# GAT's two sum tables laid out by a node's place in its block

## The chip, the cores and the metric

The kernel runs on one core of a Trainium2 chip. The metric is the device time of one execution in microseconds (us), from the first instruction to the last; lower is better. Three timed runs before the change gave 3942.16, 3943.05 and 3946.96 us, a median of 3943.05. One more execution was profiled, and the profile's lines are of that one.

A core has a matrix engine (PE; PEld is its loading of weights), a vector engine (DVE), a scalar engine (ACT), GpSimd (POOL) and SyncE (SP). Each works through its own queue of instructions in order. Transfers (DMAs) are issued from the queues of SP, ACT and POOL and carried by 16 DMA engines that all queues share.

## The reference, cut to what matters

A graph of 3125 nodes and 103125 edges passes through a layer norm, three GIN layers and a residual, then through a second layer norm and a diffusion block of three graph attention (GAT) layers with 8 heads. The change concerns the GAT layers alone. Each of them computes, for every node, a softmax over its incoming edges and the weighted sum of its neighbours' rows:

```python
xw = (x @ W).reshape(n_nodes, H, C)
logits = jax.nn.leaky_relu(al_s[src] + al_d[dst], LRELU_SLOPE)
m = jax.lax.stop_gradient(jax.ops.segment_max(logits, dst, num_segments=n_nodes))
e = jnp.exp(logits - m[dst])
denom = jax.ops.segment_sum(e, dst, num_segments=n_nodes)
alpha = e / denom[dst]
out = jax.ops.segment_sum(alpha[:, :, None] * xw[src], dst, num_segments=n_nodes)
```

A linear term of the layer's input is added, the result is normalized over all nodes, and a SiLU follows. The layers give 256, 256 and 128 features (D), with H = 8.

## The kernel before

Nodes are cut into NT = 25 blocks of Q = 125. A tile holds one block with a node on each partition, so "place in the block" is the partition. `search` and `slots` sort the graph at run time, and everything after that lies in `fast`, behind a branch on whether the graph fits.

**Index building (`slots`).** For each pair of blocks at most one edge per node goes into a regular part; the edges left over are kept per node in up to 48 slots (`RMAX`). For those, nodes are ranked by how many they have, and `perm` (L997) holds, for each rank, the node's number. Numbers of 3125 and more mark ranks without a node. Beside this, L961 on DVE builds the dense adjacency 1000 columns at a time into tiles `a`, with PE and ACT ahead of it, and ACT's queue stores them (`adj_rows`). After the last store POOL scatters left-over weights into `adj` with 400 indirect DMAs (L1015), and the GIN layers read the table.

**A GAT layer (`gat`).** It projects the nodes, stores a table of rows for gathering (`tab`) and the dense term (`dense`), and then calls `add_edges`, which forms two partial sums for each node, each with its own maximum and denominator (2H statistics):

- The regular part. For block t, with the nodes on the partitions, the sum goes into tile `o1`, and ACT's queue stores its 125 rows to the DRAM table `res` (L1330), which lies by node number. Its statistics stay on chip in `stat`.
- The left-over part. POOL gathers rows by `idx`; the sums of 128 ranked nodes and their statistics form `o2`, of D + 16 columns. POOL scatters its rows by `perm` to the DRAM table `more` (L1306 puts the scatter on a list), which also lies by node number.

Within `add_edges` the order of instructions is the order of the code (`manual_schedule`). Everywhere else a planner orders the instructions of each engine when the program is built.

**The close of a layer (`close_rows`).** ACT's queue reads the second sum's statistics from `more` into `back` (L1359). DVE combines them with `stat` (L1362 to L1371) into two factors for each node and head. Then, for seven groups of four blocks (the last has one), SP's queue loads four rows per partition from `res` and from `more` into `got1` and `got2` (L1380, four buffers each) and the dense term (L1388, eight buffers). DVE multiplies both by their factors (L1382) and adds them (L1385), PE adds the dense term (L1390) and the transposed sums (L1392) in PSUM, ACT copies to `xt` (L1396) and DVE takes statistics (L1397), once for each 128 features. Nothing of the next layer starts before the last statistics are there.

The loads and stores go through `by_rows` (L59 to L65), which issues one DMA for the first 112 of 125 partitions and a second one for the last 13; in the profile they all have the line L65. In the tables before, node (t, p) is row t * 125 + p, so the four rows that a partition needs lie 125 rows apart, and each is a piece of its own:

```python
res, more = (a[:N].rearrange("(t p) d -> p t d", p=Q) for a in (res, more))
by_rows(nc.scalar, back, more[:, :, D:])
...
        by_rows(nc.sync, a[:, :n], part[:, t0 : t0 + n, :D])
```

Of the kernel before, what the change touches and what calls it, by code (L numbers as in the profile page):

```python
# [10 lines left out]
F32 = mybir.dt.float32  # L11
BF16 = mybir.dt.bfloat16
I32 = mybir.dt.int32
AF = mybir.ActivationFunctionType
ALU = mybir.AluOpType
AX = mybir.AxisListType
# [3 lines left out]
P = 128  # L20
N = 3125
E = 103125
NT = 25
Q = 125
NP = NT * P
# [34 lines left out]
def by_rows(engine, out, in_):  # L60

    even = out.shape[0] // 16 * 16
    for rows in (slice(0, even), slice(even, out.shape[0])):
        if rows.start < rows.stop:
            engine.dma_start(out[rows], in_[rows])  # L65
# [559 lines left out]
class Fast(Base):  # L625
# [146 lines left out]
    def slots(self):  # L772


        nc, tc = self.nc, self.tc
        keep = self.keep
        self.perm = keep.tile([P, NT], I32, name="perm")
        self.idx = keep.tile([P, NT, RMAX], I32, name="idx")
        self.void = keep.tile([P, NT, NT + 1], F32, name="void")
# [15 lines left out]
        with tc.tile_pool(name="slots", bufs=1) as sp, tc.tile_pool(name="slots_ps", bufs=1, space=PSUM) as ps:  # L795
# [65 lines left out]
            for t, c in enumerate(spans):  # L861
                if t % 5 == 0:
                    keys(t, t + 5)
                n = CAPS[t]
# [11 lines left out]
            more = sp.tile([P, NT], F32, name="more")  # L876
# [38 lines left out]
            for t0 in range(0, NT, 4):  # L915
                n = min(4, NT - t0)
# [30 lines left out]
            with tc.tile_pool(name="build", bufs=1) as sp:  # L947

                for s in range(NT):
                    a = sp.tile([P, N], F32, name="a", bufs=3)[:Q]  # L950
                    for c0 in range(0, N, 8 * Q):
                        cols = [(c, min(4 * Q, N - c)) for c in range(c0, min(c0 + 8 * Q, N), 4 * Q)]
                        at = sp.tile([P, 2, 4 * Q], BF16, name="at_src", bufs=3)[:Q]
                        w = ps.tile([P, 2, BLK], F32, name="w", bufs=2)[:Q]
                        for i, (c, n) in enumerate(cols):
                            p = ps.tile([P, BLK], F32, name="by", tag="by", bufs=2)[:Q, :n]
                            nc.tensor.matmul(p, pick[0][:, s], by_src[:, c : c + n], start=True, stop=True)
                            nc.scalar.copy(at[:, i, :n], p)
                            nc.tensor.matmul(w[:, i, :n], pick[1][:, s], by_src[:, c : c + n], start=True, stop=True)
                        k = len(cols)  # L960
                        nc.vector.scalar_tensor_tensor(  # L961
                            a[:, c0 : c0 + k * n].rearrange("p (k n) -> p k n", k=k), at[:, :k, :n], self.own[:Q],
                            w[:, :k, :n], op0=ALU.is_equal, op1=ALU.mult,
                        )
                    by_rows(nc.scalar, self.adj_rows[s * Q : (s + 1) * Q], a)


                rows = sp.tile([P, NT, 2 * RMAX + 1], F32, name="rows_at")
                nc.sync.dma_start(rows, rows_d.rearrange("(t p) f -> p t f", p=P))
                there, vals, nodef = rows[:, :, :RMAX], rows[:, :, RMAX : 2 * RMAX], rows[:, :, 2 * RMAX]  # L970
                spare = sp.tile([P, NT, RMAX], F32, name="spare")
                for t in range(NT):
                    nc.gpsimd.iota(
                        spare[:, t], pattern=[[P, RMAX]], base=N * N + sum(MORE[:t]) * P, channel_multiplier=1,
                        allow_small_or_imprecise_dtypes=True,
                    )
                shape = [P, NT, RMAX]
                cell = sp.tile(shape, F32, name="cell")
                nc.vector.tensor_scalar(cell, there, -1.0, float(N), op0=ALU.add, op1=ALU.mult)
                nc.vector.tensor_tensor(cell, cell, nodef[:, :, None].to_broadcast(shape), op=ALU.add)  # L980
                nc.vector.tensor_sub(cell, cell, spare)
                some = sp.tile(shape, F32, name="some")

                nc.vector.memset(some[:, :, RMAX - 1], 0.0)
                nc.vector.tensor_tensor(
                    some[:, :, : RMAX - 1], there[:, :, : RMAX - 1], there[:, :, 1:], op=ALU.is_gt
                )
                nc.vector.tensor_mul(cell, cell, some)
                for t in range(NT):
                    m0 = sum(MORE[:t])  # L990
                    c = slice(m0, m0 + MORE[t])
                    nc.vector.tensor_tensor(celli[:, c], cell[:, t, : MORE[t]], spare[:, t, : MORE[t]], op=ALU.add)
                    nc.vector.tensor_copy(val[:, c], vals[:, t, : MORE[t]])
                    for q in range(c.start, c.stop):
                        self.scatter(self.adj, [(val[:, q : q + 1], celli[:, q : q + 1])], "adj")

                nc.vector.tensor_copy(self.perm, nodef)  # L997
                nc.vector.tensor_scalar(some, there, 0.0, float(N + 1), op0=ALU.is_equal, op1=ALU.mult)
                nc.vector.scalar_tensor_tensor(self.idx, there, -1.0, some, op0=ALU.add, op1=ALU.add)

# [88 lines left out]
    def gat(self, layer, K, D, xt, yt, ready):  # L1089


        nc, tc = self.nc, self.tc
        C, W, KO = D // H, D + H, D // P
        name = lambda n: f"L1_gnn_{n}{layer}"
        tab = tc.dram_tile([N + 1, W], F32, name=f"tab{layer}")
        ald_d = tc.dram_tile([NP, H], F32, name=f"ald{layer}")
        dense = tc.dram_tile([KO, P, NP], F32, name=f"gat_dense{layer}")
        res = tc.dram_tile([NP, D], F32, name=f"gat_res{layer}")
        more = tc.dram_tile([NP, D + 2 * H], F32, name=f"gat_more{layer}")
        with ExitStack() as ctx:  # L1100
            pool = ctx.enter_context(tc.tile_pool(name=f"gat{layer}", bufs=1))
# [10 lines left out]
            with tc.tile_pool(name=f"gat_sum{layer}", bufs=2) as io:  # L1112
                with tc.tile_pool(name=f"gat_ps_a{layer}", bufs=3, space=PSUM) as ps:
                    S = 4
                    for t0 in range(0, NT, S):
                        n = min(S, NT - t0)
                        ready(t0, n)
                        for t in range(t0, t0 + n):
                            p = ps.tile([P, BLK], F32, name="pw", tag="mm")[:Q, : W + H]
# [10 lines left out]
                    for c0 in range(0, N, BLK):  # L1130
                        w = min(BLK, N - c0)
                        for ko in range(KO):
                            p = ps.tile([P, BLK], F32, name="p1", tag="mm")
# [5 lines left out]
                            d = io.tile([P, BLK], F32, name="dense")  # L1139
# [9 lines left out]
    def add_edges(self, io, ps, layer, D, xt, yt, xw, ald, stat, tab, ald_d, res, more):  # L1149

        nc = self.nc
# [151 lines left out]

        def end_others(t, o, pa):
            nc.scalar.copy(o[:, :D], pa)
            late.append((more, [(o, self.perm[:, t : t + 1])], None))  # L1306


        load(0)
# [5 lines left out]
        for t in range(NT):  # L1315
            ahead = t + 1 < NT
            if t + 2 < NT:
                load(t + 2)
            nxt = parts(t + 1) if ahead else []
            pa = ps.tile([P, D], F32, name="pa1", tag="pa1")[:Q]  # L1320
            for i in range(3):
                if i == 1:

                    weighed = sum_others(copies - 8)
                if ahead:
                    gather(t + 1, *nxt[i])
                add_part(pa, e, *now[i])
            o = io.tile([P, D], F32, name="o1")[:Q]
            nc.scalar.copy(o, pa)
            by_rows(nc.scalar, res[t * Q : (t + 1) * Q], o)  # L1330
            added = weighed and add_others(*weighed)
            if ahead:
                now, e = nxt, weigh(t + 1, nxt)
            if added:
                end_others(*added)
# [18 lines left out]
    def close_rows(self, pool, io, ps, D, yt, stat, back, dense, res, more, bg, bb):  # L1354

        nc = self.nc
        C, KO = D // H, D // P
        res, more = (a[:N].rearrange("(t p) d -> p t d", p=Q) for a in (res, more))
        by_rows(nc.scalar, back, more[:, :, D:])  # L1359
        den1, top1, den2, top2 = stat[:, :, :H], stat[:, :, H:], back[:, :, :H], back[:, :, H:]  # L1360
        m = pool.tile([P, NT, H], F32, name="m")[:Q]
# [12 lines left out]
        for b, t0 in enumerate(range(0, NT, 4)):  # L1374
            n = min(4, NT - t0)
            c0, w = t0 * Q, n * Q
            given = []
            for name, part, s in (("got1", res, top1), ("got2", more, top2)):
                a = io.tile([P, 4, D], F32, name=name, bufs=4)[:Q]
                by_rows(nc.sync, a[:, :n], part[:, t0 : t0 + n, :D])  # L1380
                v = a[:, :n].rearrange("p t (h c) -> p t h c", c=C)
                nc.vector.tensor_tensor(v, v, s[:, t0 : t0 + n, :, None].to_broadcast([Q, n, H, C]), op=ALU.mult)  # L1382
                given.append(a)
            a = given[0]
            nc.vector.tensor_add(a[:, :n], a[:, :n], given[1][:, :n])  # L1385
            for ko in range(KO):
                d = io.tile([P, BLK], F32, name="dense", bufs=8)
                nc.sync.dma_start(d[:, :w], dense[ko, :, c0 : c0 + w])  # L1388
                p = ps.tile([P, BLK], F32, name="p1", tag="mm")
                nc.tensor.matmul(p[:, :w], self.ident, d[:, :w], start=True, stop=False)  # L1390
                for i in range(n):
                    nc.tensor.matmul(  # L1392
                        p[:, i * Q : (i + 1) * Q], a[:, i, ko * P : (ko + 1) * P], self.ident[:Q, :Q], start=False,
                        stop=i == n - 1,
                    )
                nc.scalar.copy(yt[ko][:, c0 : c0 + w], p[:, :w])  # L1396
                nc.vector.bn_stats(stats[:, ko, b], p[:, :w])  # L1397
# [132 lines left out]
```

## Time and profile before

| what | value |
|---|---|
| median of three runs | 3943.05 us |
| profiled execution | 3936.36 us |
| its span, first to last instruction | 3934.5 us |
| mean granted PE clock | 0.791 |
| busy: PE, DVE, POOL, ACT | 2175.0, 2211.1, 2011.1, 866.9 us |
| DMA | 557.74 MB, 142 GB/s over the span |
| first close, from `back`'s issue to its last statistics | 2318.0 to 2375.4 us |
| second close | 3159.5 to 3220.3 us |
| third close | 3873.6 to 3907.0 us |

All times inside the execution count from the start of the span. A line of the timeline gives start and length in us, the engine with the source line, the operation, what it writes and reads with shapes, how many were merged, and in brackets the idle time before it and what ended that. SPq and ACTq are the DMA issues of those queues: their length is the time that the queue took to issue, not the transfer. A line of the waits gives who waited, for what, the sum in us, how often, and the longest. Two lines of the page show how even the load is and where DMA stands over the span's 40 slices of 98 us:

```profile
PE 2175.0 (55%) x9841; PEld 1566.1 (40%) x9841; DVE 2211.1 (56%) x3558; ACT 866.9 (22%) x2127; POOL 2011.1 (51%) x1916
...
DMA  3000496960019993644444364555444356444323
```

### The profile page before, as it was taken

How to read it: one execution, taken by the hardware profiler on the slowest of the kernel's cores; microseconds unless marked ns; L12 is line 12 of the kernel's file. 1: busy time of each engine (PE TensorE's matmuls, PEld its weight loads, DVE VectorE, ACT ScalarE, POOL GpSimd, SP SyncE). 2: the span in 40 equal slices, each digit the busy share in tenths (PEclk: the TensorE clock that was granted, in tenths of full speed). 3: DMA queues.
4: the chain of work that ended last, by engine and by line, in shares of the span. 5: the costliest groups of instructions: out<-in, count | busy, mean ns of one | idle time of the engine just before them, and what ended most of it. 6: DMA issues, size and time to landing. Idle time of an engine off the chain costs nothing. (4 is left out here: it accounts for less than half of the span.)

```text
span 3934.5 us, 32038 instructions
## 1 busy us (share of the span) xinstructions
PE 2175.0 (55%) x9841; PEld 1566.1 (40%) x9841; DVE 2211.1 (56%) x3558; ACT 866.9 (22%) x2127; POOL 2011.1 (51%) x1916
## 2 busy tenths in 40 slices
PE   1001352000019997788898638788998355676533
PEld 0000120000003333567676525666776245665532
DVE  7799864210000002388898743788898553676544
ACT  0001353000000002333433204333443022222111
POOL 4512307677750000457667731476677704777772
PEclk8555685555559997899999868999999677888765
DMA  3000496960019993644444364555444356444323
GB/s 131 12 14 6 150 297 143 272 200 0 1 50 372 356 368 122 184 134 152 148 144 145 99 142 157 106 162 162 144 158 112 96 124 162 138 137 137 103 54 77
DMA packets 224866, 557.74 MB, mean 142 GB/s; under 512 B 90249, under 2 KB 135057, under 8 KB 208843
## 3 DMA queue, kind: packets, MB, share of 16 engines
q1 hardware_dynamic: 112634, 307.69, 23.8%
q0 software_dynamic: 74800, 158.73, 16.1%
q10 hardware_dynamic: 37250, 89.18, 7.4%
q8 instruction: 80, 1.31, 0.1%
q14 instruction: 102, 0.84, 0.1%
HBM read 439.37 MB, written 116.05 MB: 141 GB/s over the span
## 5 line engine op out<-in xcount | busy, mean ns | idle before, releaser
L1023 POOL DMA_INDIRECT rows<-tab,idx x1200 | 1266.5, 1055 | 626.6 <-issue 271.4
L1015 POOL DMA_INDIRECT adj<-val,celli x400 | 423.7, 1059 | 302.1 <-DMA gw<-in_L_gnn_gat_w 149.8
L1051 PE MATMUL pa<-adj_t,h 125*64 125x500 f32 (+1 forms) x1050 | 269.7, 554 | 511.5 <-DMA adj_t<-adj 510.8
L1221 PE MATMUL pa<-xt,ident 125*125 125x256 f32 (+1 forms) x1800 | 395.6, 376 | 239.4 <-DVE xt L1219 194.7
L1171 PE MATMUL g<-xw,hot 125*125 125x264 f32 (+1 forms) x2400 | 498.7, 360 | 37.5 <-ACT xt L1174 37.5
L1174 ACT COPY xt<-g 125x528 f32<-125x528 f32 (+1 forms) x700 | 439.8, 636 | 303.5 <-PE g L1171 296.5
L1221 PEld LDWEIGHTS pa<-xt,ident 125*125 125x125 f32 x1800 | 323.0, 212 | 302.9 <-DVE xt L1219 196.5
L1171 PEld LDWEIGHTS g<-xw,hot 125*125 125x125 f32 x2400 | 387.3, 192 | 128.1 <-ACT xt L1174 83.4
L1212 DVE TENSOR_TENSOR xt<-xt,le 125x3072 f32<-125x3072 f32 (+1 forms) x150 | 421.6, 2811 | 0.0
L1299 PE MATMUL pa<-rows,ident 128*128 128x256 f32 (+1 forms) x1236 | 289.1, 388 | 230.7 <-issue 186.7
L1023 POOL DMA_INDIRECT at<-ald,perm x75 | 74.7, 996 | 622.1 <-DMA ald<-ald 414.8
L170 DVE TENSOR_TENSOR h<-p,L_gnn_b 125x256 f32<-125x256 f32 (+1 forms) x21 | 8.3, 395 | 644.1 <-PE p L168 611.9
L1051 PEld LDWEIGHTS pa<-adj_t,h 125*64 125x64 f32 x1050 | 86.7, 137 | 673.8 <-issue 578.2
L1299 PEld LDWEIGHTS pa<-rows,ident 128*128 128x128 f32 x1236 | 228.9, 217 | 283.3 <-issue 194.9
L1171 PE MATMUL g<-xw,xt 125*125 125x264 f32 (+1 forms) x1350 | 289.5, 370 | 57.5 <-ACT xt L1174 32.8
L1212 DVE TENSOR_TENSOR rows<-rows,le 128x2048 f32<-128x2048 f32 (+8 forms) x180 | 292.8, 1627 | 0.0
L1171 PEld LDWEIGHTS g<-xw,xt 125*125 125x125 f32 x1350 | 226.1, 199 | 109.8 <-ACT xt L1174 59.3
L1219 DVE TENSOR_TENSOR xt<-xt 125x1536 f32<-125x1536 f32 (+1 forms) x150 | 223.8, 1492 | 5.1
L1351 ACT ACTIVATE le<-le 125x208 f32<-125x208 f32 (+16 forms) x147 | 42.9, 292 | 659.2 <-DVE le L1350 645.1
L1281 DVE TENSOR_TENSOR le<-rows,at 128x64 f32<-128x64 f32 (+4 forms) x162 | 35.9, 222 | 261.6 <-DMA rows<-tab,idx 224.8
L1063 ACT COPY gin_acc<-pa 128x500 f32<-128x500 f32 (+1 forms) x21 | 10.2, 531 | 770.9 <-DMA adj_t<-adj 523.6
L1297 DVE TENSOR_TENSOR rows<-rows 128x1024 f32<-128x1024 f32 (+5 forms) x174 | 157.0, 902 | 6.0
(268 smaller groups left out, 2779.3 us busy)
## 6 DMA issues: line engine op xcount, KB each, us to landing
hot<-hot SPq DMA_DIRECT2D x48, 1562.5 KB
adj_t<-adj SPq DMA_DIRECT2D x144, 500.0 KB
adj_t<-adj SPq DMA_DIRECT2D x72, 562.5 KB
xt<-hot SPq DMA_DIRECT2D x24, 1562.5 KB
adj<-a ACTq DMA_DIRECT2D x25, 1367.2 KB
hot<-one ACTq DMA_DIRECT2D x25, 1367.2 KB
rows<-tab,idx POOLq DMA_INDIRECT x1200
row<-lane_d SPq DMA_DIRECT2D x25, 683.6 KB
```

Of the source, the lines that this page charges most:

```text
L1015: st = self.nc.gpsimd.indirect_dma_start(out=table, out_offset=bass.IndirectOffsetOnAxis(ap=idx, axis=0), in_=row, in_offset=None)
L1023: self.nc.gpsimd.indirect_dma_start(out=out, out_offset=None, in_=table, in_offset=bass.IndirectOffsetOnAxis(ap=idx, axis=0))
L1051: nc.tensor.matmul(pa[i * D0 : (i + 1) * D0, c // B, :w], h[:, s], tiles[i][:, c : c + w], start=s0 == 0, stop=s0 + i >= NT - 2 and i == 1,)
L1171: nc.tensor.matmul(g[:Q, j // k, j % k * W : (j % k + 1) * W], one, xw[:, t if s == NT else s], start=True, stop=True)
L1174: nc.scalar.copy(rows[:, i : i + m].rearrange("p (b k) w -> p b k w", k=k), g[:Q, :banks, : k * W].rearrange("p b (k w) -> p b k w", w=W),)
L1212: nc.vector.tensor_tensor(r, r, e[:, s0 : s0 + n, :, None].to_broadcast([*r.shape[:3], C]), op=ALU.mult)
L1219: nc.vector.tensor_add(rows[:, :m, :D], rows[:, :m, :D], rows[:, m:n, :D])
L1221: nc.tensor.matmul(pa, self.ident[:Q, :Q], rows[:, j, :D], start=s0 + j == 0, stop=s0 + n == NS and j == m - 1)
L1281: nc.vector.tensor_tensor(l[:, k0 : k0 + n], rows[:, :n, D:], at[:, None, :].to_broadcast([P, n, H]), op=ALU.add)
L1297: nc.vector.tensor_add(rows[:, : n - m, :D], rows[:, : n - m, :D], rows[:, m:n, :D])
L1299: nc.tensor.matmul(pa, self.ident, rows[:, k, :D], start=k0 + k == 0, stop=k0 + n == MORE[t] and k == m - 1)
L1351: nc.scalar.activation(e, l, AF.Exp)
```

## The change

Row numbers in both tables are turned round: node (t, p) becomes row p * 25 + t. `res` is declared as [Q, NT, D], and block t is stored to `res[:, t]`, a row of D numbers every 25 rows. The scatter to `more` uses new row numbers, `turned`. They are made once in `slots` from the node number n: with t the number of multiples of 125 up to n, the new row is n + 24 n - 3124 t, which is 25 (n - 125 t) + t; numbers from 3125 on stay. In the close, the four rows of a partition are then adjacent in memory. For `more` the load takes whole rows with their 16 statistics columns, so that they stay one piece, and the tile `got2` grows to D + 16 columns, of which the first D are used. `back` is still read as 16 columns of each row.

```diff
+        self.turned = keep.tile([P, NT], I32, name="turned")
...
                 nc.vector.tensor_copy(self.perm, nodef)
+
+                bounds = sp.tile([P, NT], F32, name="bounds")
+                nc.gpsimd.iota(bounds, pattern=[[Q, NT]], base=Q, channel_multiplier=0, allow_small_or_imprecise_dtypes=True)
+                past = some[:, :, :NT]
+                nc.vector.tensor_tensor(
+                    past, nodef[:, :, None].to_broadcast([P, NT, NT]), bounds[:, None, :].to_broadcast([P, NT, NT]),
+                    op=ALU.is_ge,
+                )
+                turned = sp.tile([P, NT], F32, name="turned_f")
+                off = sp.tile([P, NT], F32, name="off")
+                nc.vector.reduce_sum(turned, past, axis=AX.X)
+                nc.vector.tensor_scalar(off, turned, -(NT * Q - 1.0), None, op0=ALU.mult)
+                nc.vector.scalar_tensor_tensor(off, nodef, NT - 1.0, off, op0=ALU.mult, op1=ALU.add)
+                nc.vector.tensor_scalar(turned, nodef, float(N), None, op0=ALU.is_lt)
+                nc.vector.tensor_mul(off, off, turned)
+                nc.vector.tensor_tensor(self.turned, nodef, off, op=ALU.add)
...
-        res = tc.dram_tile([NP, D], F32, name=f"gat_res{layer}")
+
+        res = tc.dram_tile([Q, NT, D], F32, name=f"gat_res{layer}")
...
-            late.append((more, [(o, self.perm[:, t : t + 1])], None))
+            late.append((more, [(o, self.turned[:, t : t + 1])], None))
...
-            by_rows(nc.scalar, res[t * Q : (t + 1) * Q], o)
+            by_rows(nc.scalar, res[:, t], o)
...
-        res, more = (a[:N].rearrange("(t p) d -> p t d", p=Q) for a in (res, more))
+        more = more[:N].rearrange("(p t) d -> p t d", p=Q)
...
-                a = io.tile([P, 4, D], F32, name=name, bufs=4)[:Q]
-                by_rows(nc.sync, a[:, :n], part[:, t0 : t0 + n, :D])
+                a = io.tile([P, 4, part.shape[2]], F32, name=name, bufs=4)[:Q]
+                by_rows(nc.sync, a[:, :n], part[:, t0 : t0 + n])
+                a = a[:, :, :D]
```

## The prediction

> **What bounds the kernel now.** No single engine does: DVE is busy 56% of the span, PE 55%, POOL 51%. The span is a chain of stages, so I read the page's 40 slices first, to find the stages, then each stage that the diff touches in the timeline, the waits and the packet records (each DMA packet's queue, size and time). Two places are touched: the end of the index building (around 457 us) and the close of each of the three GAT layers, where `res` and `more` are read back (2318 to 2376, 3159 to 3222, 3874 to 3907 us). First, what the DMA engines do there, beside a stretch of GIN (start:end, length, busy of PE, PEld, DVE, ACT, POOL, then PE clock, DMA share, GB/s):
>
> ```profile
> 1180.00:1300.00 120.00, 110.61 (x500) 43.17 (x497) 4.73 (x14) 7.70 (x14) 0.00 (x0) 1.00 0.99 369
> 2318.00:2363.00 45.00, 22.26 (x85) 14.35 (x86) 27.53 (x33) 5.25 (x10) 0.00 (x0) 0.73 1.05 219
> 3159.00:3204.00 45.00, 22.95 (x82) 14.90 (x82) 22.73 (x29) 5.07 (x10) 0.00 (x0) 0.64 1.02 218
> 3873.00:3898.00 25.00, 12.76 (x42) 7.27 (x42) 14.53 (x26) 2.94 (x6) 0.00 (x0) 0.65 0.97 201
> ```
>
> The DMA engines are full in each close, at 201 to 219 GB/s, where GIN's 4000-byte rows get 369. That looks like the thing to mend. But who waits for these loads? The waits of the second close, and one line of the whole run's:
>
> ```profile
> PEld p L1392 <- DVE got L1385: 23.3, 6, 6.6
> ...
> DVE stats L1397 <- ACT xt L1396: 15.0, 10, 2.7
> ...
> DVE m L1362 <- DMA back<-gat_more: 51.2, 3, 19.5
> ```
>
> DVE waits for ACT, PE for DVE, and DVE for one transfer only, `back`, once a layer. It never waits for `got`. The timeline of the first close says why:
>
> ```profile
> 2346.08 1.22 DVE L1385 TENSOR_TENSOR got<-got,got 125x1024 f32<-125x1024 f32 x1
> ...
> 2347.36 1.29 PEld L1392 LDWEIGHTS p<-ident,got 125*128 125x128 f32 x8 [4.56 <-DVE got L1385]
> ...
> 2348.98 0.57 ACT L1396 COPY xt<-p 128x500 f32<-128x500 f32 x1 [5.60 <-PE p L1392]
> ...
> 2352.55 0.69 DVE L1397 BATCH_NORM_STATS2 stats<-p 128x6 f32<-128x500 f32 x1 [2.28 <-ACT xt L1396]
> 2353.16 1.21 DVE L1382 TENSOR_TENSOR got<-got,back 125x1024 f32<-125x1024 f32 x1
> ```
>
> Add, transposes, copy, statistics, and only then the next block's second multiply: 7.5 us a block (two blocks from 2340.7 to 2355.7), in the fixed order of DVE's queue. By the packet records the loads arrive every 6.7 us: `got` of blocks 1, 3 and 5 is in at 2333.9, 2346.9 and 2360.5, and its second multiply runs at 2338.2, 2353.2 and 2369.0. The loads are 4 to 9 us ahead, and pull further ahead. **So a close lasts from the landing of `back` to the end of a chain of DVE, PE and ACT; the `got` loads are hidden.** What sets `back` is seen in the second layer:
>
> ```profile
> 3159.49 2.53 ACTq L65 DMA_DIRECT2D back<-gat_more  x2
> 3159.59 1.06 SPq L65 DMA_DIRECT2D got<-gat_res  x2
> 3160.70 0.85 SPq L65 DMA_DIRECT2D got<-gat_more  x2
> 3161.60 0.98 SPq L1388 DMA_DIRECT2D dense<-gat_dense  x2
> 3165.32 0.83 SPq L65 DMA_DIRECT2D got<-gat_res  x2
> ...
> 3170.15 0.37 DVE L1362 TENSOR_TENSOR m<-stat,back 125x200 f32<-125x200 f32 x1 [19.47 <-DMA back<-gat_more]
> ```
>
> 200 KB in 64-byte pieces take 10.7 us, with SP's loads beside them; in layers 0 and 2 it is 7.2 and 6.6 us.
>
> **Part 1, reads of `res` and `more` (L1380).** Removed: three of four packets. Per full block and table 500 rows of 1024 bytes (512 in layer 2) become 125 of 4096 and 4352 (2048 and 2304). The DMA count stays (two per load), SP's issue time (about 0.45 us each) with it; `more` brings its 16 statistics columns, 6% more bytes. [...] By the rows it is 0, since nobody waits for them. I take 0 for the gain; the multiplies keep their 1.22 us, as their element count is unchanged (the added stride of 272 in `got2` is bounded by 0 and 0.1 us an instruction; I take 0).
>
> **Part 2, what the larger packets do to `back`.** This is the unknown cost. Of `back`'s 3125 packets (11 ns each) most pass before SP's first packet; the rest share each of the 16 engines with SP's. I counted per engine, from SP's first packet to `back`'s last. Layer 0: 40 of `back`, about 40 of SP, 3.75 us; layer 1: 137 and 88 in 7.8 us; layer 2: 159 and 67 in 3.7 us. In all three the time is their own 11 ns times the count plus SP's packets at their own durations (1024 bytes median 71 to 74 ns, 512 bytes 34, 2000-byte `dense` 133): 137 x 11 + 88 x 71 = 7.8 us. So `back` waits for SP packet by packet, and larger packets cost it more. [...] The trace has no 4096-byte read in this stage: the nearest are GIN's 4000 bytes at 155 ns, and four times the 72 ns of here, 290. With the same number of SP packets let in between:
> - layer 0: 24 large and 16 `dense` at 133, 24 x (155 to 290) + 16 x 133 + 40 x 11 = 6.3 to 9.5 us instead of 3.75: +2.5 to +5.8;
> - layer 1: 44 large and 44 `dense`: 12.7 to 18.7 us instead of 6.3: +6.4 to +12.4;
> - layer 2: 44 of 2048 bytes (85 to 150 ns) and 23 `dense`: 5.6 to 9.6 instead of 2.0: +3.6 to +7.6.
> If SP gets the same bytes rather than the same packets, it is 0. [...] I take +3, +5 and +2.5, between equal bytes and equal packets, since layers 1 and 2 already show fewer than one SP packet for one of `back`. Behind the waiting L1362 in DVE's queue stands the whole close, so this goes to the span in full. `back` itself is still 3125 rows of 64 bytes.
>
> **Part 3, writes.** `res[:, t]` still goes out as 1024-byte rows from ACT's queue, 50 issues a layer at 0.36 us; only the pitch in memory grows. The last one is long done when the close begins, and its buffer is reused a block later (some 25 us). 0; without that cover, a few us on ACT. The scatter to `more` has other row numbers, the same 75 instructions: 0.
>
> **Part 4, building `turned`.** One compare of 128 x 625 (0.8 us, between 0.69 for 512 and 1.22 for 1024 elements), one sum over it (0.7 us), five on 25 columns (0.08 to 0.17 us each as they follow one another in the rows of L992): 2.2 us on DVE, and one iota on POOL (0.17 us), whose queue is idle from 429 to 580 us. They come beside `perm`:
>
> ```profile
> 457.04 0.17 DVE L997 CAST perm<-rows_at 128x25 int32<-128x25 f32 x1
> ...
> 458.44 2.67 DVE L961 SCALAR_TENSOR_TENSOR a<-at_src,own,w 125x1000 f32<-125x1000 bf16 x3
> 459.73 0.27 PE L959 MATMUL w<-by_src,pick 128*125 128x125 bf16 x1 [8.28 <-DVE a L961]
> ```
>
> PE already waits 8.3 us for DVE here. DVE is busy 99 of the 120 us of this stage, and the last `a` releases the scatters to `adj` at 579.8, which POOL issues one by one until 1168, and GIN waits for them. So 2.2 us on the path; 0 if the writes of `adj` absorb them.
>
> **Sum.** 2.2 + 3 + 5 + 2.5 = +12.7 us. The profiled execution took 3936.4 us (span 3934.5 and 1.9 around it); the median of the runs is 6.7 us above it. 3943.05 + 12.7 = 3955.7 us, +0.3%.
>
> **Rivals.**
> - Nothing reaches the path: SP gets equal bytes, or the four rows still travel as four packets, so that the change doesn't do what it says. Only part 4 stays: 3945. For it: DVE's wait list has no `got`. Against: the packet counts above.
> - `back` lands sooner, because SP's queue runs dry between fewer, faster packets and lets it through. [...] It decides once `back` takes under some 6 us a layer. For it: in layer 1 over a thousand of `back`'s packets rush through in 1 us (3164 to 3165) when SP pauses. Against: in all layers its tail crawls whenever SP is busy.
> - The order changes: outside of the hand-ordered sums a planner fixes each queue, and the new shapes may move a multiply before or behind the statistics. DVE is busy for only some 36 of the first close's 56 us, so it could give 10 us a layer or take as much: 3925 to 3985. The trace can't tell.
>
> **How the numbers follow.** A measurement of this kernel can't tell less than about 0.2% (8 us) from no change. Forecast 0.48, nine tenths of it above +8 us; nothing reaches the path 0.28, where part 2's low ends leave 0.05 above +8; `back` sooner 0.10, half of it beyond -8; the order changes 0.14, shared evenly between both signs. Slower 0.43 + 0.05 + 0.07 = 0.55; faster 0.05 + 0.07 = 0.12; the rest, 0.33, within. The range, 3937 to 3973, goes from a small gain of `back` to the high ends of layers 0 and 1 with a middling layer 2; the likeliest case's own range is 3949 to 3973.
>
> **What would show it.** Right: DMA packets of 4096 and 4352 bytes, GB/s in the closes well above 219, the SP loads far ahead, the wait of L1362 above 51.2 us in sum, and unchanged 7.5 us a block behind it. Wrong: `back` landing within 5 us; or DVE's order of multiply and statistics different; or L1382 waiting for `got`, which would mean that I misread what hides the loads; or scatters to `adj` starting at 580 as before (part 4).

## The result, and the profile after

| | before | after |
|---|---|---|
| median of 13 runs each, taken together | 3948.67 us | 3955.11 us |
| lowest to highest | 3942.16 to 3955.41 | 3950.95 to 3968.26 |
| ratio | | 1.002 (95%: 1.001 to 1.0029) |
| profiled execution, span | 3934.5 us | 3953.3 us |

The changed kernel is slower by 0.2%, some 4 to 11 us, just measurably. The two profiles lie 18.8 us apart, more than the typical runs do: the profiled run of before was faster than each of its 13 timed ones.

What the DMA engines do after, in a stretch of GIN and in the three closes (windows of the same kind and length as those shown of before):

```profile
1190.00:1310.00 120.00, 110.81 (x493) 42.81 (x494) 4.73 (x14) 7.71 (x14) 0.00 (x0) 1.00 0.99 365
2330.00:2375.00 45.00, 22.14 (x82) 14.24 (x82) 24.02 (x30) 5.25 (x10) 0.00 (x0) 0.73 0.91 223
3176.00:3221.00 45.00, 21.05 (x82) 13.58 (x82) 24.96 (x31) 5.25 (x10) 0.00 (x0) 0.72 0.93 223
3890.00:3915.00 25.00, 11.48 (x32) 6.10 (x32) 13.39 (x24) 2.38 (x5) 0.00 (x0) 0.58 0.82 206
```

The packets are indeed four times as large (by the packet records 4096 and 4352 bytes, 2048 and 2304 in layer 2), yet the closes move 206 to 223 GB/s, as before (201 to 219). The share of busy DMA fell from about 1.0 to 0.82 to 0.93, so the engines have some slack, and nobody uses it. Who waits, over the whole run:

```profile
PEld p L1411 <- DVE got L1404: 60.1, 17, 6.4
DVE m L1380 <- DMA back<-gat_more: 54.8, 3, 19.1
```

The wait for `back` grew from 51.2 to 54.8 us, and there is still no wait of DVE for `got`. Where `back` sits in the first close (timeline of after; L1380 was L1362):

```profile
2330.01 2.96 ACTq L65 DMA_DIRECT2D back<-gat_more  x2
2330.82 1.01 SPq L65 DMA_DIRECT2D got<-gat_res  x2
2331.87 0.79 SPq L65 DMA_DIRECT2D got<-gat_more  x2
2332.70 1.07 SPq L1407 DMA_DIRECT2D dense<-gat_dense  x2
...
2340.17 0.37 DVE L1380 TENSOR_TENSOR m<-stat,back 125x200 f32<-125x200 f32 x1 [19.05 <-DMA back<-gat_more]
```

Issued at 2330.01, used at 2340.17: 10.16 us, where before had 7.21. And behind it the chain of a block, DVE alone, in the same close:

```profile
2352.24 0.69 DVE L1416 BATCH_NORM_STATS2 stats<-p 128x6 f32<-128x500 f32 x1 [0.65 <-ACT xt L1415]
2352.84 1.21 DVE L1401 TENSOR_TENSOR got<-got,back 125x1024 f32<-125x1024 f32 x1
2354.09 1.22 DVE L1404 TENSOR_TENSOR got<-got,got 125x1024 f32<-125x1024 f32 x1
2357.16 0.69 DVE L1416 BATCH_NORM_STATS2 stats<-p 128x6 f32<-128x500 f32 x1 [1.86 <-ACT xt L1415]
```

It is the order of before: statistics, multiply, add, and a pause for PE and ACT. The second multiplies of blocks 1, 3 and 5 start 7.2, 23.1 and 38.1 us after that of block 0; before it was 7.6, 22.6 and 38.4.

By stage, from milestones in both traces (us; `back` from its issue to `m`, a close from `m` to the last statistics):

| | before | after |
|---|---|---|
| `perm` to the end of the last `a` | 111.8 | 119.3 |
| `back`, layers 0, 1, 2 | 7.21, 10.66, 6.57 | 10.16, 10.03, 7.80 |
| close, layers 0, 1, 2 | 50.20, 50.15, 26.82 | 49.89, 50.09, 26.85 |

Index building +7.5 and `back` +3.6 are places that the change touches. The other 8 of the 18.8 us lie mostly in the scatters to `adj`, GIN and the sums (last scatter minus first gather of a layer: 745.0 to 744.7, 744.9 to 747.3, 623.6 to 624.7).

### The profile page after: what moved, and what is told of

It reads as the page before. It is cut to its first block, busy times and chain, and to the rows that moved or that the text cites. A ratio compares the mean times of both kernels' runs of the same rounds, so it can differ in the third digit from the quotient of the medians.

```text
span 3953.3 us, 32046 instructions
## 1 busy us (share of the span) xinstructions
PE 2171.6 (55%) x9841; PEld 1562.0 (40%) x9841; DVE 2214.0 (56%) x3565; ACT 868.6 (22%) x2127; POOL 2012.4 (51%) x1917
```

## The experiments

They ran on four other chips, where the kernel before takes 4217 to 4249 us: a layer's sums are longer there (from first gather to `back`'s issue 842 us in e1's first layer, 747 before). So ratios are taken to the kernel before on the same chip, and the text goes by the stages above. The changed kernel itself was not timed there. Each run left one trace, and a close of the same instructions differs between traces by up to 1.8 us (first layer: 50.20 before, 48.42 in e1), so a single difference below that says little.

**e1, e2: one part of the change alone.** e1 is the kernel before, which also builds `turned` and does not use it. e2 is the changed kernel without `turned`: it scatters by `perm`, and so adds the second sums of other nodes.

```diff
 e1, before:  + self.turned and the eight instructions that fill it
 e2, after:
-            late.append((more, [(o, self.turned[:, t : t + 1])], None))
+            late.append((more, [(o, self.perm[:, t : t + 1])], None))
```

> The kernel before, with the new row numbers computed but not used: only part 4 of the change. My theory (the numbers cost DVE time in a stage that is DVE's): the last tile of the adjacency is ready 3.6 us or more later than in the kernel before (2.2 us of operations and some 1.4 us in which PE and ACT, let run dry, refill), the scatters start as much later, and the whole takes +4 to +8 us, half or more of what the change costs. Rival (the later stores absorb it, the 7.9 us between the two profiles are chance): the scatters start within 1 us of before and the time is the same within 2 us.

> The changed kernel without its new row numbers: both tables have the new shape and are read in large pieces, but the second sum is scattered by the old numbers, so it is read for other nodes; the work is the same. My theory (back waits behind SP's packets, larger ones hold it longer): back takes 10 us or more in layer 0, 10 in layer 1, 7.5 to 8 in layer 2 instead of 7.2, 10.7 and 6.6, the chain behind it keeps its 50, 50 and 27 us, and the time is +2 to +6 us. Rival (the faster loads gain something, hidden by part 4): the closes are shorter than in the kernel before and the time is below it.

Measured: e1 0.9993 (0.9973 to 1.0012), e2 1.0 (0.9983 to 1.0018). The +4 to +8 us that e1 was to add to the whole did not show (the interval is -11 to +5 us), and e2's +2 to +6 can't be told from nothing (-7 to +8): the whole cannot tell parts of a few us here; the stages can. `perm` to the last `a`: e1 115.1 us, e2 111.2. `back`: e1 7.26, 10.73, 7.77 and e2 11.21, 9.61, 8.04, so the layout gives +3.1 in sum and all of it in layer 0. The closes of e2 (50.21, 48.87, 27.91) are in sum no shorter than those of before (127.0 and 127.2 us). The numbers cost something in index building, the layout in `back`, and neither gains.

**e3, e4: `back` ahead of the loads in SP's own queue**, in the kernel before and in the changed one.

```diff
-        by_rows(nc.scalar, back, more[:, :, D:])
+        by_rows(nc.sync, back, more[:, :, D:])
```

> The kernel before, with back loaded from SP's queue ahead of got instead of from ACT's. My theory (back is held up by SP's packets that are served in turn): ahead of them in one queue it lands about 5 us after its issue in every layer instead of 7.2, 10.7 and 6.6, the 50, 50 and 27 us behind it stay or grow by 1 to 2 where got now comes later, and the time falls by 4 to 9 us. Rival (64-byte pieces are slow by themselves, or the memory is): back takes as long as before, got lands later, and the time is the same or a few us more.

> The changed kernel, with back loaded from SP's queue ahead of got. My theory: back lands about 5 us after its issue instead of 10.2, 10.0 and 7.8, whatever the size of the packets behind it; got, faster than in the small pieces, is there when DVE has the factors; the time falls by 8 to 13 us below the changed kernel. Rival (packets play no part): no change against the changed kernel.

Measured: e3 0.9968 (0.9946 to 0.9989), e4 0.9981 (0.9967 to 0.9995). The timeline of e3's first close:

```profile
2416.81 1.94 SPq L65 DMA_DIRECT2D back<-gat_more  x2
2419.25 0.82 SPq L65 DMA_DIRECT2D got<-gat_res  x2
...
2420.57 0.37 DVE L1362 TENSOR_TENSOR m<-stat,back 125x200 f32<-125x200 f32 x1 [11.69 <-DMA back<-gat_more]
```

`back` takes 3.76, 3.67, 3.47 us in e3 and 4.17, 4.01, 3.95 in e4, less than the 5 us expected, whatever stands behind it: three to seven microseconds of its time before and after were SP's packets. The closes grow by 0.6 to 2.0 us (51.90, 52.11, 27.46 in e3): the first loads are issued 2.4 us behind `back`, and DVE now waits 1.1 us for `got` in e3's first close. The 8 to 13 us below the changed kernel that e4 was to gain can't be read, as that kernel was not timed on this chip; by the stages of the traces, `back` and the closes together take 11.8 us less in e4 than in the changed kernel. The new row order costs `back` 0.4 us a layer even alone.

**e5, e6: the statistics of a block behind the next block's multiplies and add**, in the kernel before and in the changed one: the close gets an order written by hand, and PSUM six buffers instead of three. It takes the wait for ACT out of DVE's queue, so that the loads may become the bound. Which of the three (the new place of the statistics, the fixed order, the buffers) was needed was not tried.

```diff
+        last = []
+        with self.tc.manual_schedule():
...
             nc.vector.tensor_add(a[:, :n], a[:, :n], given[1][:, :n])
+            for a_, b_ in last:
+                nc.vector.bn_stats(a_, b_)
...
-                nc.vector.bn_stats(stats[:, ko, b], p[:, :w])
+                mine.append((stats[:, ko, b], p[:, :w]))
+            last = mine
```

> The kernel before, with each block's statistics moved behind the next block's two multiplies and add in DVE's queue (hand-ordered close, six PSUM buffers instead of three). It takes away the chain of add, transposes, copy and statistics that I hold for the bound of the close (7.5 us a block). My theory: DVE could then do a block in 5.0 us, and the loads, which need 6.7 us a block in small pieces, become the bound: DVE waits for got, and the time from the factors' start to the last statistics falls from 50 to 44 to 47 us in layers 0 and 1, from 27 to 22 to 25 in layer 2; -8 to -14 us in all. Rival (the loads were the bound already): 50 us stay.

> The same edit in the changed kernel. If large pieces make the loads faster once somebody waits for them: the closes fall to 36 to 40 us in layers 0 and 1 (DVE's 5.0 us a block) and DVE does not wait for got. If the rate is the memory's and not the pieces' (the close of the changed kernel showed 225 to 250 GB/s, with 4096 bytes in 225 ns): they fall to 43 to 46, about as in the kernel before with this edit, and DVE waits for got.

Measured: e5 0.9971 (0.9952 to 0.9989), e6 0.9956 (0.9939 to 0.9972). Closes: e5 43.91, 41.50, 22.82; e6 37.40, 39.78, 22.07, as expected or a little shorter. The chain was the bound, by 6 to 12 us in the first two layers. The large pieces now give 6.5 and 1.7 us in the closes, of which `back` takes 3.7 back in layer 0. DVE in e5's second close, where a block takes 4.7 us:

```profile
3366.27 1.23 DVE L1387 TENSOR_TENSOR got<-got,got 125x1024 f32<-125x1024 f32 x1
3367.41 1.26 DVE L1389 BATCH_NORM_STATS2 stats<-p 128x6 f32<-128x500 f32 x2
3368.59 1.21 DVE L1384 TENSOR_TENSOR got<-got,stat 125x1024 f32<-125x1024 f32 x1
3369.72 1.22 DVE L1384 TENSOR_TENSOR got<-got,back 125x1024 f32<-125x1024 f32 x1
3370.97 1.23 DVE L1387 TENSOR_TENSOR got<-got,got 125x1024 f32<-125x1024 f32 x1
...
3378.60 1.22 DVE L1384 TENSOR_TENSOR got<-got,stat 125x1024 f32<-125x1024 f32 x1 [0.52 <-DMA got<-gat_res]
3381.23 1.23 DVE L1384 TENSOR_TENSOR got<-got,back 125x1024 f32<-125x1024 f32 x1 [1.40 <-DMA got<-gat_more]
```

There is no pause in the first five lines. At this pace I estimate a close at 35 us (4.3 of factors, 6.25 blocks of 4.7, 1.3 of last statistics). e5's takes 41.5, with 5.0 us of waits for ACT at its ends and, in the last two lines, 1.9 for `got`: the loads have come within sight.

**e7, e8: both edits together.** e7 is e5 with `back` on SP's queue. e8 is e6 with it, and there GpSimd builds the new numbers with nine small instructions on 25 columns.

> The kernel before with both edits: statistics late, and back loaded from SP's queue ahead of got. If the gains add: back 3.5 to 4 us after its issue, closes as with late statistics plus 1 to 2 us since got now starts behind back; 12 to 22 us below the kernel before.

> The changed kernel with both edits and with the new row numbers made by eight small operations on POOL (block number by rounding, no 25-wide compare), which stands idle there. My theory: the last tile of the adjacency and the scatters are as early as in the kernel before (within 1 us; it was +3.3 us with the numbers on DVE), back lands within 4.5 us, and the closes are those of the changed kernel with late statistics plus 1 to 2 us; 15 to 35 us below the kernel before, by whether large pieces load faster. Rival for the numbers: POOL's operations cost DVE time too, and +3 us stay.

Measured: e7 0.9955 (0.9929 to 0.9981), e8 0.9954 (0.9933 to 0.9975). The two gains don't add up: with `back` in front, the closes are 46.87, 48.14, 25.39 and 45.93, 46.09, 25.53, 2.6 to 8.5 us longer than in e5 and e6, where 1 to 2 were expected. Waits in e8's first close:

```profile
PE p L1411 <- DMA dense<-gat_dense: 19.8, 5, 13.5
...
DVE got L1400 <- DMA got<-gat_more: 4.9, 5, 1.1
DVE got L1400 <- DMA got<-gat_res: 2.4, 5, 0.6
```

Now DVE does wait for `got`. The loads bind, at 254, 237 and 235 GB/s (SP's bytes from its first to its last packet), against 229, 229 and 226 with small pieces in e7. So it is not the pieces that hold the rate there. With the numbers on GpSimd, `perm` to the last `a` takes 110.2 us.

**e9 to e12: loads that cover 128 partitions in one DMA** instead of 112 and 13 in two. The three rows more are zeros or belong to no node, and are not used.

```diff
-                    a = io.tile([P, 4, part.shape[2]], F32, name=name, bufs=4)[:Q]
-                    by_rows(nc.sync, a[:, :n], part[:, t0 : t0 + n])
-                    a = a[:, :, :D]
+                    a = io.tile([P, 4, part.shape[2]], F32, name=name, bufs=4)
+                    nc.sync.dma_start(a[:, :n], part[:, t0 : t0 + n])
+                    a = a[:Q, :, :D]
```

e9 is e6 with it, e10 is e5 with it (rows t * 125 + p for p up to 127, pieces of 1024 bytes), e11 is e8 with it, and e12 is e7 with it.

> The changed kernel with the statistics late (e6), and in it the `got` loads cover 128 partitions in one DMA instead of 112 and 13 in two (the three added rows are zeros or rows that no node has, and are not used). Beside e6 (closes 37.4, 39.8 and 22.1 us, SP's stream 240, 219 and 214 GB/s). Theory A, the rate of 200 to 250 GB/s is that of loads which cover 125 partitions unevenly, as GIN's loads of 128 rows get 369: the stream goes above 300 GB/s and the closes fall to what DVE's own work takes, some 33 to 35 us in layers 0 and 1 and 19 to 20 in layer 2. Theory B, the rate is that of reading these tables, or of the dense loads beside them, whatever the rows: closes and rate within 1.5 us and 5% of e6.

> The kernel before with the statistics late (e5), and in it the `got` loads cover 128 partitions in one DMA, still in pieces of 1024 and 512 bytes (three rows more, that are not used). Beside e5 (closes 43.9, 41.5 and 22.8 us, 232, 222 and 210 GB/s). If the uneven cover alone sets the rate: above 300 GB/s as in e9, closes within 2 us of e9's. If the pieces begin to count once the cover is even: e9 is faster in its closes by over 4 us a layer in layers 0 and 1. If neither counts: as e5 within 1.5 us.

> e9 with `back` ahead of the loads on SP's queue and the new numbers made by GpSimd (e8 with loads of 128 partitions). If the rate rises in e9, back and close together take some 40, 40 and 24 us (e8: 50.0, 50.2 and 29.5), about 25 us less in all than e8, and the ratio to the kernel before is near 0.990. If the rate doesn't rise: as e8, 0.995.

> e10 with `back` ahead of the loads on SP's queue: the kernel before, its small pieces and its numbers, with the statistics late and loads of 128 partitions; e11 without the change itself. If the layout brings nothing once the loads cover 128 partitions: back 3.5 to 3.8 us, closes 36 to 37.5 us in layers 0 and 1 and 22 in layer 2 as in e11 (35.9, 37.1 and 22.0), ratio to the kernel before 0.988 to 0.992. If large pieces pay by then: the stream stays near the 302 to 313 GB/s of e10 where e11 has 365, closes 2 to 4 us longer than e11's in layers 0 and 1, and ratio 0.990 to 0.993.

| | ratio (95%) | `back` | close | GB/s in layers 0, 1 |
|---|---|---|---|---|
| e9, large | 0.9944 (0.9922 to 0.9967) | 11.47, 11.15, 8.85 | 36.87, 36.93, 22.01 | 290, 283 |
| e10, small | 0.9935 (0.9918 to 0.9951) | 8.57, 9.38, 7.03 | 36.53, 36.70, 22.77 | 313, 302 |
| e11, large, `back` first | 0.989 (0.9848 to 0.9932) | 4.12, 4.06, 4.16 | 35.87, 37.14, 22.01 | 365, 367 |
| e12, small, `back` first | 0.9893 (0.9861 to 0.9926) | 3.87, 3.70, 3.70 | 36.82, 36.77, 22.07 | 336, 329 |

One DMA over 128 partitions lifted the limit (e9's 290 and 283 GB/s where e6 has 240 and 219); larger pieces had not (e5 has 232 and 222). (e9's direction was foreseen, its size less so: over 300 GB/s and closes of 33 to 35 us were expected in the first two layers.) Median time of a packet in the first layer (ns, from the packet records):

```
              112 + 13 partitions    128 partitions
1024 bytes    74 (e5)                47 (e10)
2000 bytes    132 (e5), 128 (e6)     88 (e10), 82 (e9)
4096 bytes    252 (e6)               159 (e9)
```

Is it the number of rows, or the second small DMA? A comparison for that stood in every trace from the start, that of before included. GIN loads `adj` with one DMA of 128 rows for a block of nodes (L71), but the last block goes through `by_rows` as 112 and 13. At the end of the third GIN layer no other load of `adj` follows those two. The trace of before, while the last loads of 128 rows pass and then while the one of 112 does:

```profile
1488.00:1493.00 5.00, 4.42 (x23) 1.38 (x20) 0.00 (x0) 0.00 (x0) 0.00 (x0) 1.00 1.01 410
1493.30:1495.30 2.00, 1.05 (x6) 0.33 (x4) 0.00 (x0) 0.00 (x0) 0.00 (x0) 1.00 0.94 208
```

By the packet records a piece of 4500 bytes takes 174 ns in the median in the loads of 128 rows, 312 in the one of 112, and 174 again in the one of 13, which passes last (the 17th to 64th piece of the 112 rows, well ahead of those last 13, take 328); in all 14 traces the three are 174, 287 to 345 and 174 to 224. So in GIN it is the load of 112 rows that is slow, and not the small one behind it. In the closes the two were not separated.

Windows of the second close, e6 and then e11, over the stretch in which the loads come:

```profile
3333.00:3373.00 40.00, 22.17 (x100) 14.61 (x100) 27.68 (x33) 6.31 (x12) 0.00 (x0) 0.74 1.01 232
```

```profile
3317.00:3343.00 26.00, 18.42 (x82) 12.23 (x82) 23.49 (x29) 4.91 (x10) 0.00 (x0) 0.75 0.99 380
...
3317.00:3353.00 36.00, 26.48 (x128) 17.83 (x128) 32.69 (x42) 7.72 (x15) 0.00 (x0) 0.82 0.72 275
```

The second line of e11 is its whole close: DVE is busy 32.7 of 36 us. It is the bound now, and closes of 36 to 37 us are its own work, with large and with small pieces. In e9 and e10 `back` is in ACT's queue still. e9's closes gain 3.4 us in sum over e6's and its `back` gives 3.3 back, while e10's gain 12.2 over e5's and its `back` loses 0.6; wide and large is the worst neighbour for `back`. e11 and e12 are 1.1% faster than the kernel before, which is the faster of the two that this is about, and they are alike: their intervals reach some 0.4% to either side, and `back` and the closes sum to 107.4 and 106.9 us. With everything out of its way the layout makes SP's stream 9 to 12% faster in the first two layers (e11 against e12) and brings nothing in time that the runs can tell.

Why 112 rows make a packet slow the runs do not show, as the records have no partitions.

## Why the prediction was right, and where not

**The forecast** was 3955.7 us, and the median is 3955.11. It is closer than its sum deserves: the base of three runs, 3943.05, lay 5.6 us below the median of 13, and the sum of +12.7 was too large by about as much. The ratio gives +4 to +11 us.

**Part 1 (reads, 0) was right.** Closes 50.20 to 49.89, 50.15 to 50.09, 26.82 to 26.85. e5 and e6 show the reason: only when the statistics are taken out of the chain do the closes shorten, and then they shorten with small pieces as well. And the prediction did not see that the rate of 219 GB/s, which I set against GIN's 369, is not one of pieces: with the loads as the bound (e7 and e8) four times larger pieces raise it by 3 to 11%, and one DMA over 128 partitions (e11 against e8) by 44 and 55% in the first two layers. Two of the signs that I named for being right did not come: GB/s well above 219 (206 to 223 in the same windows), and loads far ahead, which by the packet records hold in layer 0 alone (8 to 16 us ahead of the second multiply, before 4 to 10; in layers 1 and 2 as before within some 3 us). They spoke of loads for which nobody waits, so the time was not touched.

**Part 2 (`back`) was right in the place and in the sign of the sum, and wrong in how the cost arises.** The term was +3, +5, +2.5; measured +2.95, -0.63, +1.23, so 3.6 instead of 10.5. Two more pairs of traces agree: e2 less e1 +3.96, -1.12, +0.27, and e6 less e5 +3.71, -0.56, +0.64. The cost is layer 0's, where I had put the largest share in layer 1. That SP's packets hold `back` up is shown by e3 and e4. What failed is the step from there to the price: that SP is let in by a count of packets, so that larger ones cost more. From the packet records, what SP's queue moved before `back`'s last packet:

```
          SP packets per engine     MB of SP          back's packets left at SP's first
          before      after         before   after    before   after
layer 0   42          28            0.69     1.44      722     2578
layer 1   86          32            1.66     1.57     2332     3125
layer 2   65          31            0.59     1.05     2391     3125
```

In layer 1 the bytes stayed and the packets fell to a third: no cost, where I took +5. In layer 0 SP got 0.75 MB more; at the 250 GB/s of SP's stream in that close they are worth 3.0 us, an estimate that matches the measured 2.95. It fits that my count had one thing as fixed which moved: who starts first. Before, three quarters of `back` had passed in layer 0 when SP's first packet came. After, `back`'s first packet comes later (1.45 us behind its issue instead of 0.97, in layer 1 2.66 instead of 0.99) and SP's first one earlier (1.17 us behind its issue instead of 1.50). No run moved the start alone, and in layer 1 a later start cost nothing, so this last step is argued and not shown. That the equal count of packets and this head start gave a cost of the same sign, and in layer 0 of the same size, is luck. By equal counts of packets I had put SP's share of layer 1's stretch at 12.7 to 18.7 us instead of 6.3; in the trace of after the whole stretch, from SP's first packet to `back`'s last, takes 8.1 us (7.9 before).

**Part 3 (writes, 0)** shows no cost in the sums, as far as a change of 2.4 us in one of three layers can tell.

**Part 4 (`turned`, +2.2) was right in place and about right in size.** The instructions themselves, timeline of after:

```profile
457.54 0.80 DVE L1003 TENSOR_TENSOR some<-rows_at,bounds 128x625 f32<-128x625 f32 x1
458.26 2.67 DVE L962 SCALAR_TENSOR_TENSOR a<-at_src,own,w 125x1000 f32<-125x1000 bf16 x3
460.85 0.80 DVE L1009 TENSOR_REDUCE turned_f<-some 128x25 f32<-128x625 f32 x1
...
464.38 0.19 DVE L1011 SCALAR_TENSOR_TENSOR off<-rows_at,off 128x25 f32<-128x25 f32 x1
...
470.36 2.64 DVE L962 SCALAR_TENSOR_TENSOR a<-at_src,own,w 125x1000 f32<-125x1000 bf16 x2 [1.48 <-ACT at_src L959]
```

Seven of them sum to 2.5 us, and the last line shows what I left out: PE and ACT, which work ahead for `a`, had waited for DVE, and DVE now waits for them (1.48 us; 0.37 at this place in the trace of before). Most of that is made up again: DVE's waits ahead of the remaining `a` sum to 19.4 us in the median of the kernels with the numbers on DVE, and to 18.9 in that of the others. `perm` to the last `a` is 115.1 us in the mean of the five kernels that build the numbers on DVE, and 111.8 in the nine that don't: +3.3, or +2.5 by the medians (114.1 and 111.6). The ranges are 113.2 to 119.3 and 110.2 to 115.3, so the 7.5 of the profiled pair is in part its own luck. The sign that I named held: scatters to `adj` start at 587.2, not 580. On GpSimd, in e8 and e11, the cost is gone (110.2 and 111.6).

So the measured terms are 2.5 to 3.3 and 3.6, some 6 to 7 us, within what the ratio says. Of the rivals, "nothing reaches the path" is out by both terms. "`back` lands sooner" happened in layer 1 alone, by 0.6 to 1.1 us in the three pairs, though a `back` that nobody holds up does land much sooner: 3.76, 3.67 and 3.47 us in e3, 13.5 us less in sum than in the profile of before. "The order changes" did not happen.

**Slips in the working** that did not decide the result: only in layer 0 do most of `back`'s packets pass before SP's first (2332 and 2391 of 3125 were left in layers 1 and 2); the low end of layer 2's sum is 44 x 85 + 23 x 133 = 6.8 us instead of 5.6, so +4.8 instead of +3.6; over a thousand packets rush through between 3163 and 3164, not 3164 and 3165; and POOL's last scatter to `adj` ends at 1155.8, not 1168.

## What to carry to other kernels

Before loads are made better, find out whether anyone waits for them: here the DMA share was 0.97 to 1.05 in three closes in which DVE never waited for the loads. When a small load with many pieces is what the next stage waits for, put it ahead of the bulk loads in their own queue; on a queue of its own they held it up here by 3 to 7 us a layer. And where a rate is low, compare the packets with the same size elsewhere in the trace before their size is blamed: here 1024 bytes took 74 ns in loads of 112 and 13 partitions and 47 in one of 128, and that was worth more than four times larger pieces. The trace of before held the same comparison in GIN, and to look there first would have told it without a run.

## What was not expected of the hardware

In layers 0 and 1, loads of 112 and 13 partitions ran at 219 to 254 GB/s where those of 128 reached 283 to 367, also with small pieces, and the 2000-byte loads of `dense` beside them, which had 128 partitions all along, fell from 132 to 88 ns a packet too. In GIN the 112 rows of the last block passed at 208 GB/s, right behind loads of 128 rows at 410. `back` alone at the head of a queue takes 0.4 us longer in the new row order (its first packet comes 1.44 us behind the issue in e11 and 0.95 in e12), though its pieces are the same 64 bytes; why, stays open.
